# Four fronts of a graph-and-mixer network on one core: norms computed in halves, nodes transposed token tile by token tile, first products in two halves of the tokens

## The chip, the core and the metric

The kernel runs on one core of a Trainium2 chip, in one launch. The metric is the device time of one execution in microseconds (us): of the kernel before, 3632.74 as the median of three (3631.09 to 3634.49). The engines are TensorE (PE for its matmuls, PEld for its weight loads), VectorE (DVE), ScalarE (ACT), GpSimd (POOL) and SyncE (SP); each has its own queue of instructions, and semaphores join them. DMAs are issued on the queues of SP and POOL.

## What is computed

A network of four layers works on 512 nodes of 768 features, in float32, with 8704 edges. Each layer is

```
xn = layernorm(x)
x  = x + graph_net(xn, edges) + mixer(xn)
x  = x + ffn(layernorm(x))
```

The graph nets, mixers and FFNs of the four layers are of different kinds. What matters here:

- **Mixer of layer 0** (8 heads of 96 features, 256 random features `rf`): `phi(q) = exp(q rf^T - |q|^2 / 2)`, the same for k, then `phi(q) (phi(k)^T v)` over `phi(q) sum(phi(k))`, and a projection. `|q|^2` and `|k|^2`, one number per node and head, are the "norms" of this text.
- **Mixer of layer 1** (12 heads of 64): the same form; its first products are those of v.
- **FFN of layer 1**, a dense block: `gelu(xn W1^T + b1) W2` with 384 hidden features.
- **Layer 3**: a graph attention of 12 heads of 64, narrow because all heads share one 64 x 64 weight `W_fc` and one `W_res`; and a linear mixer with 768 queries, keys and values, normalized along the tokens, and a projection. Its FFN has 16 experts, each of which takes its 64 best nodes, with gate, up and down weights of 768 x 3072, and a shared block.

## The kernel before, in words

x stays in SBUF as 4 token tiles of 128 nodes (`NT` = 4). A product over features needs the nodes with the features on the partitions: `xnT`, 6 chunks of 128 features by 512 nodes (`KC` = 6, `N` = 512). PE makes them by transposes of 128x128, and DVE or ACT copy them out of PSUM. PSUM has eight banks of 128x512 floats, handed out in turn by `ps()`.

A planner sets the order of each engine's queue: the order of the Python code is the priority, and of two instructions the earlier one goes first unless its inputs are ready later by the planner's own clock. So a piece of Python code that is run "beside" another, by a generator that is advanced by one step per product, lands between that code's instructions. `issue_after` adds an order by hand. Weights come on SP's queue (`w`, L299), into six rotating buffers in most stages. Small loads come on POOL's.

Helpers: `copy` (L286 to L292) gives copies to DVE (L290) and ACT (L292) in turn; `acc` (L429) is a row of accumulating matmuls; `tr` (L450) is one transpose; `norm1` (L505 to L517) the layernorm of one token tile: two bn_stats, aggregate, square root on ACT, reciprocal, and a scaling on DVE of 128x768. `add_x` (L522) adds a product of 128x384 to x on DVE.

`to_fm` (L457 to L464) turns the nodes: token tile by token tile, 24 transposes into six banks, one per chunk of features, then six copies of 128x512. Each copy needs the transposes of all four tiles, and a product needs all six copies. It is called for the second mixer (L2799), in the dense block (L1958) and for the last layer (L2300).

**First mixer** (`mix0`, L817). Its 8 heads go in two groups g of four. Products of the first layers are made from slices of float32 split in parts (rounded on ACT by `cut`, L2069, and the rest), for accuracy. For each group `heads3` makes the keys of four heads by four products (48 matmuls) and calls a function beside the first three of them, then the same for the queries. `norms` (L847 to L858) handles four heads: ACT squares (L852) and rounds (L2069), DVE subtracts (L854), PE sums over the 96 features by two matmuls per head (L856), and four copies (L858) put the rows into row 96 of `qk`, where the later products pick them up. The keys' norms are run as one piece beside the first query product; the queries' norms come behind all query products and the `keys` of two heads (L860: matmuls with `rf`, exponentials on ACT). Then `queries` (L870) and the rest of each head go in a pipeline. `part` and `sq` have two buffers.

In group 0, between the products of keys and queries, stands `checked` (L687 to L704), which looks whether the graph's counts are in the expected bounds: two DVE reductions, a row of matmuls for the degrees (`deg`), 4 times two DVE instructions which add the degrees to the diagonal of `AT`, then one small product `ones` by `check` and four more small DVE instructions (L700 to L704), the last of which writes `big`. SP loads `big` into registers (L923) in group 1; a branch later depends on it.

**Second mixer** (`mix1`): after `to_fm` at L2799 and the short `turn`, the products of v are made by token tiles: for weight block 4, then 5, all six chunks of one token tile at a time.

**Dense block** (`ffn1`, L1952): norm, `to_fm`, then three chunks of hidden features, each by six matmuls of 512 columns over six chunks (the trace has 36 matmuls, as each is done in two passes), GELU on ACT, and the second product.

**Last layer** (`last_two`, L2291). After `to_fm`, `gnn3` (the graph attention, L2380) is created as a generator of 41 steps, and its opening runs at once: loads on POOL's queue (among them the block-diagonal `bd` of `W_fc` and `W_res`), the narrow product of the attention's vectors `V`, 24 products of nodes with `bd` and their copies. Its other steps are advanced by two per product. The products are `fm(m3_wqkv, ...)`: nbs 0 to 3 are queries and keys, 12 products of 512 columns, each followed by `put` (L2310: ACT copies with sums, and two steps of `gnn3`); then the queries are scaled, nbs 4 and 5 are the values (6 products), and the projection goes by token tiles, two products of 384 columns per tile, with two steps after each. Where the generator has ended, the rows of the finished tiles are normed and written to DRAM (L2352, L2353), from where the experts' nodes are fetched.

The experts' weights use SP's queue from the end of `last_two` on: `ffn3` (L2461) takes some of its buffers from the SBUF that `gnn3` used, so SP waits there for the last instruction of `gnn3` that reads this memory, `add` (L2445).

Of the kernel before, what the change touches and what calls it, by code (L numbers as in the profile page):

```python
# [10 lines left out]
F32 = mybir.dt.float32  # L11
BF16 = mybir.dt.bfloat16
F32R = mybir.dt.float32r
# [9 lines left out]
P = 128  # L23
N = 512
NT = N // P
D = 768
KC = D // P
HW = 384
# [177 lines left out]
class Net:  # L206
# [250 lines left out]
    def to_fm(self, x, out):  # L457
# [5 lines left out]
        for f in range(KC):  # L463
            self.copy(out[:, f, :], ps[f])  # L464

    def to_fm_last(self, x, out):

        nc, cut = self.nc, (NT - 1) * P
        ps = [self.ps() for _ in range(KC)]
# [3 lines left out]
        for f in (0, 1, 3, 4):  # L473
            i = nc.scalar.copy(out[:, f, :cut], ps[f][:, :cut])
# [3 lines left out]
        for f in range(0, KC, 3):  # L478
            p = self.ps()
# [5 lines left out]
            else:  # L485
                with self.tc.issue_after(i.ins):
                    i = nc.scalar.copy(*at)
# [80 lines left out]
    def counts(self, AT, EFT, deg, tmp, ones, meanwhile, then):  # L568
# [10 lines left out]
        with ExitStack() as c:  # L579
# [88 lines left out]
            for f in range(2):  # L668
                p = self.ps()
# [17 lines left out]
        def checked():  # L687
# [8 lines left out]
            for t in range(NT):  # L696
                at = slice(t * P, (t + 1) * P)
                nc.vector.tensor_mul(tmp, self.ident, deg[:, at])
                nc.vector.tensor_add(AT[:, t, at], AT[:, t, at].bitcast(F32), tmp)
            p = self.ps()  # L700
            self.acc(p[:, :5], [(self.ones, check)])
# [115 lines left out]
    def mix0(self, xnT, checked, ops, v, bv):  # L817
# [3 lines left out]
        with ExitStack() as c:  # L821
# [25 lines left out]
            def norms(qk, s):  # L847
                p = self.ps()
                for h in range(4):
                    sq = two.tile([96, N], F32, name="sq")  # L850
                    part = two.tile([96, 2, N], F32R, name="part")
                    nc.scalar.activation(sq, qk[:96, s, h, :], AF.Square)  # L852
                    self.cut(part[:, 0], sq)
                    nc.vector.tensor_sub(part[:, 1], sq, part[:, 0].bitcast(F32))  # L854
                    for i in range(2):
                        nc.tensor.matmul(p, half[:, 96 - 32 * h : 224 - 32 * h], part[:, i], start=h + i == 0, stop=h + i == 4)  # L856
                for h in range(4):
                    self.copy(qk[96:97, s, h, :], p[32 * h : 32 * h + 1])  # L858
# [62 lines left out]
            for g in range(2):  # L921
                if g:
                    loads, (self.wrong,) = nc.values_load_multi_w_load_instructions(self.big[:1], min_val=0, max_val=1)  # L923
                qk = one.tile([97, 2, 4, N], F32, name="qk")
                self.heads3(d["m0_wqkv"][2 + g, 0], ops, qk[:96, 1], sb[:, KC + 3 * g : KC + 3 * g + 3], scale,
                            lambda i: next(left, None))
                if g == 0:
                    checked()
                self.heads3(d["m0_wqkv"][g, 0], ops, qk[:96, 0], sb[:, 3 * g : 3 * g + 3], scale,
                            lambda i: norms(qk, 1) if i == 0 else None)  # L930
                fks = [keys(qk, 0), keys(qk, 1)]
                norms(qk, 0)
                fq = queries(qk, 0)
# [1018 lines left out]
    def ffn1(self):  # L1952
        nc, tc, d = self.nc, self.tc, self.d
        with tc.tile_pool(name="f1", bufs=1) as one:
            xn = one.tile([P, NT, D], F32, name="xn")
            xnT = one.tile([P, KC, N], F32, name="xnT")
            self.norm(self.x, xn)
            self.to_fm(xn, xnT)  # L1958
            w1, w2 = self.wk(d["f1_w1"]), self.wr(d["f1_w2"])
            hT = one.tile([P, 3, N], F32, name="hT")  # L1960
            for f in range(3):
                p = self.ps()
                self.acc(p, [(w1[:, k, f * P : (f + 1) * P], xnT[:, k, :]) for k in range(KC)])
                nc.scalar.activation(hT[:, f, :], p, AF.Gelu, bias=self.col("f1_b1", f))
# [326 lines left out]
    def last_two(self, xn, xnT, out, V):  # L2291
# [5 lines left out]
        with ExitStack() as c:  # L2297
            one = c.enter_context(tc.tile_pool(name="m3_one", bufs=1))
            two = c.enter_context(tc.tile_pool(name="m3_two", bufs=2))
            self.to_fm(xn, xnT)  # L2300
            beside = self.gnn3(c, xnT, V)
            next(beside)
            qk = one.tile([P, 2, KC, N], F32, name="qk")
# [16 lines left out]

            self.fm(d["m3_wqkv"], xs, put, nbs=(0, 1, 2, 3))
            nc.scalar.activation(rn, s[:, 1], AF.Sqrt)
# [413 lines left out]
def tile_net(ctx, tc, dram, at, out, only=ALL):  # L2736
# [51 lines left out]
    with tc.tile_pool(name="L1", bufs=1) as pool, ExitStack() as keep:  # L2788
# [9 lines left out]
        nc.gpsimd.memset(V1, 0.0)  # L2798
        net.to_fm(xn, xnT)  # L2799
        turn(V1, vt)  # L2800
# [51 lines left out]
```

## Time and profile before

| | before |
|---|---|
| median of 3 runs | 3632.74 us |
| the profiled execution | 3629.75 us |
| its span, first to last instruction | 3628.0 us |
| PE busy | 97% |
| DVE, ACT, POOL busy | 47%, 27%, 13% |
| granted TensorE clock, mean | 0.991 |
| DMA | 714.56 MB, mean 197 GB/s |

Where the four places lie in the span (us from its start):

| place | from | to | what the ends are |
|---|---|---|---|
| mixer 0, group 0: keys' products | 114.4 | 126.6 | matmuls of `heads3` |
| mixer 0, group 0: queries' products | 130.2 | 144.9 | matmuls of `heads3` |
| mixer 0, group 0: norms of the queries | | 153.5 | first matmul behind them |
| mixer 1: transposes | 939.6 | 946.8 | `to_fm` at L2799 |
| mixer 1: first product | 948.4 | | |
| dense block: transposes | 1491.8 | 1497.7 | `to_fm` at L1958 |
| dense block: first products | 1497.8 | 1513.5 | 36 matmuls |
| last layer: transposes | 2305.5 | 2313.4 | `to_fm` at L2300 |
| last layer: first product of `m3_wqkv` | 2330.0 | | |
| `gnn3` ends | | 2490.3 | `add`, L2445 |
| last layer: projection ends | | 2511.4 | |
| last matmul of the experts | | 3608.9 | |

How to read the views. A row of a timeline has the start and the length of an instruction or a group of like ones, engine, line and operation, output <- inputs, partitions x elements, how many (x4), and in brackets the idle time of the engine before it with the instruction that ended the wait. A row of the windows has the stretch, its length, then for PE, PEld, DVE, ACT and POOL the busy time and the number of instructions, the mean granted TensorE clock (1.00 is full speed), the mean busy share of the DMA engines and the GB/s that they moved. In a list of waits, the numbers are the total in us, how often, and the longest.

### The profile page before, as it was taken

The page shows a single profiled execution, that of the slowest core. Times are in us where ns is not written, and L with a number is a line of the kernel's source. Part 1 is how long each engine was busy: PE and PEld are TensorE (multiplying, and loading weights), DVE is VectorE, ACT ScalarE, POOL GpSimd, SP SyncE. Part 2 cuts the span into 40 slices and gives each one's busy share as a digit, 9 for nine tenths or more (in the row PEclk, how much of TensorE's full clock was granted, in tenths as well). Part 3 has the DMA queues.
Part 4 walks back from the last instruction along what each step waited for, and adds up shares of the span by engine and source line. Part 5 has one row for each costly group of instructions (what it writes and reads, how often), then busy time and mean ns, then how long its engine had stood idle before and what let it go on. Part 6 is the DMA issues. An engine that isn't in the chain of part 4 may idle for free.

```text
span 3628.0 us, 40612 instructions
## 1 busy us (share of the span) xinstructions
PE 3530.9 (97%) x15976; PEld 2208.5 (61%) x15981; DVE 1707.9 (47%) x3422; ACT 980.6 (27%) x1741; POOL 475.2 (13%) x522
## 2 busy tenths in 40 slices
PE   8999999999999999999999998999999999999998
PEld 6668666655586675587878785556444444444444
DVE  8647664653433662366777763476222221221211
ACT  2533332332342453142343432263000000000000
POOL 8211110012003010001221213111000000000000
PEclk9999999999999999999999998999999999999999
DMA  4213122228312120022121118415999999999998
GB/s 177 91 49 119 43 87 90 72 94 335 111 68 92 71 114 35 0 109 100 54 90 66 66 40 310 149 53 211 389 423 424 424 424 424 424 424 423 424 425 351
DMA packets 96988, 714.56 MB, mean 197 GB/s; under 512 B 11744, under 2 KB 12000, under 8 KB 27280
## 3 DMA queue, kind: packets, MB, share of 16 engines
q1 hardware_dynamic: 76032, 604.81, 41.3%
q0 software_dynamic: 16848, 95.99, 6.9%
q10 hardware_dynamic: 3904, 11.01, 0.8%
q8 instruction: 132, 2.16, 0.2%
q14 instruction: 72, 0.59, 0.0%
HBM read 689.22 MB, written 22.54 MB: 196 GB/s over the span
## 4 chain that ended last, share of the span: by engine, by line
PE 64%; DMA 5%; DVE 3%; issue 1%; ACT 0%; POOL 0%; POOLq 0%; DVEq 0%; SPq 0%; ACTq 0%
PE ps L429 29%; PE ps L2655 12%; PE ps L2671 7%; PE ps L2175 6%; PE ps L2626 3%; DMA w<-in_f_Wd_dram 2%; PE ps L450 2%; PE ps L1888 2%; PE ps L400 1%; DMA w<-in_f_Wg_dram 1%; DMA w<-in_f_Wu_dram 1%; PE ps L1869 1%; DVE pt L1598 1%; DVE e L1597 1%; DMA xb<-f_there,who 0%
## 5 line engine op out<-in xcount | busy, mean ns | idle before, releaser
L2655 PE MATMUL ps<-w,xg 128*64 128x384 f32 x3072 | 565.3, 489 | 7.7 <-DMA w<-in_f_Wg_dram 4.3
L2655 PEld LDWEIGHTS ps<-w,xg 128*64 128x64 f32 x3072 | 236.8, 137 | 295.6 <-issue 262.7
L429 PE MATMUL ps<-ops,w 128*128 128x512 f32 x1584 | 383.8, 392 | 0.0
L429 PEld LDWEIGHTS ps<-ops,w 128*128 128x128 f32 x1584 | 296.2, 188 | 63.6 <-issue 1.9
L2671 PE MATMUL ps<-w,hT 128*64 128x384 f32 x1536 | 320.6, 490 | 3.3 <-DMA w<-in_f_Wd_dram 1.9
L2175 PE MATMUL ps<-ops,w 128*128 128x512 f32 x1080 | 259.4, 390 | 1.3 <-DVE xn L2184 0.6
L2069 ACT ACTIVATE w<-w 128x768 fp32r<-128x768 f32 (+1 forms) x192 | 156.6, 825 | 355.9 <-PE ps L429 269.4
L2658 ACT ACTIVATE h<-ps 128x384 f32<-128x384 f32 x64 | 31.4, 491 | 795.8 <-PE ps L2655 795.8
L2671 PEld LDWEIGHTS ps<-w,hT 128*64 128x64 f32 x1536 | 134.3, 137 | 162.0 <-issue 136.3
L2175 PEld LDWEIGHTS ps<-ops,w 128*128 128x128 f32 x1080 | 201.9, 188 | 45.8 <-ACT ops L2088 1.7
L522 DVE TENSOR_TENSOR x<-x,ps 128x384 f32<-128x384 f32 x232 | 127.1, 552 | 188.9 <-PE ps L429 179.8
L2659 DVE TENSOR_TENSOR h<-h,ps 128x384 f32<-128x384 f32 x64 | 35.5, 554 | 354.4 <-PE ps L2655 345.8
L2113 DVE TENSOR_TENSOR w<-w,w 128x768 fp32r<-128x768 f32 x174 | 166.0, 957 | 65.1 <-ACT w L2069 61.8
L429 PE MATMUL ps<-w,xnT 128*128 128x384 f32 x564 | 189.4, 489 | 0.0
L429 PE MATMUL ps<-w,hT 128*128 128x384 f32 x552 | 184.6, 490 | 2.8 <-ACTq L1474 2.8
L2083 POOL TENSOR_TENSOR low<-low,ops 128x512 f32<-128x512 f32 x90 | 118.4, 1316 | 422.9 <-ACT ops L2069 422.9
L2114 DVE SCALAR_TENSOR_TENSOR w<-w 128x768 fp32r<-128x768 f32 x174 | 170.8, 984 | 3.2
L429 PEld LDWEIGHTS ps<-w,hT 128*128 128x128 f32 x552 | 103.1, 190 | 80.4 <-ACT xbT L292 7.1
L429 PEld LDWEIGHTS ps<-w,xnT 128*128 128x128 f32 x564 | 106.9, 191 | 73.5 <-issue 5.7
L2626 PE MATMUL ps<-xnT,sw 128*128 128x512 f32 x288 | 135.4, 603 | 0.0
L429 PE MATMUL ps<-C,parts 128*128 128x512 f32 x576 | 132.5, 389 | 0.0
L2090 DVE TENSOR_TENSOR ops<-ops 128x512 fp32r<-128x512 f32 x138 | 123.6, 906 | 16.4 <-ACT ops L2088 16.0
(585 smaller groups left out, 5188.8 us busy)
## 6 DMA issues: line engine op xcount, KB each, us to landing
w<-in_f_Wg_dram SPq DMA_DIRECT2D x128, 1152.0 KB, 22.5
w<-in_f_Wu_dram SPq DMA_DIRECT2D x128, 1152.0 KB, 22.4
w<-in_f_Wd_dram SPq DMA_DIRECT2D x128, 1152.0 KB, 22.4
w<-in_g_w_dram SPq DMA_DIRECT2D x54, 1152.0 KB, 5.1
w<-in_m_wqkv_dram SPq DMA_DIRECT2D x16, 1152.0 KB, 6.0
w<-in_g_t_dram SPq DMA_DIRECT2D x12, 1152.0 KB, 5.0
w<-in_m_wp_dram SPq DMA_DIRECT2D x11, 1152.0 KB, 5.0
ea<-in_attr_dram SPq DMA_DIRECT2D x17, 512.0 KB, 4.7
```

Source lines behind the costliest of these rows:

```text
L429: i = self.nc.tensor.matmul(out, a, b, start=n == 0, stop=n == len(pairs) - 1)
L450: return self.nc.tensor.transpose(out, in_, self.ident[:k, :k])
L522: self.nc.vector.tensor_add(xs, xs, p)
L2069: return self.nc.scalar.activation(top, x, AF.Copy, scale=CUT).ins
L2083: (engine or nc.gpsimd).tensor_sub(low, v, ops[:, 0, k, :].bitcast(F32))
L2090: nc.vector.tensor_sub(dif, top.bitcast(F32), x.bitcast(F32))
L2113: nc.vector.tensor_sub(low, w, top.bitcast(F32))
L2114: self.sliced_last = nc.vector.scalar_tensor_tensor(dif, low.bitcast(F32), -TIMES, top.bitcast(F32), OP.mult, OP.add).ins
L2175: nc.tensor.matmul(outs[o], w[:, i, k], ops[:, i, k, :], start=n == 0 and i + k == 0, stop=n == 4 and i + k == KC)
L2626: i = nc.tensor.matmul(p, w[:, k, :], xnT[:, k, :], start=k == 0, stop=k == KC - 1)
L2655: nc.tensor.matmul(p[a * 64 : a * 64 + 64, :HW], xg[:, k, a * CAP : (a + 1) * CAP], ws[b][a][:, k, :], start=k == 0, stop=k == KC - 1)
L2671: nc.tensor.matmul(po[nb][a * 64 : a * 64 + 64, :HW], hT[:, f * P + a * 64 : f * P + a * 64 + 64], wd[a][:, f, nb * HW : (nb + 1) * HW], s ...
```

## The change

`to_fm_tiles` stands in for `to_fm` at its three calls: each token tile is transposed in two groups of three chunks, and one copy of 128x384 follows each group, so that there are eight copies instead of six.

`in_halves` makes three output chunks of a product in three banks that are held together: first the first 256 tokens of all three, then the other 256. It replaces the first products of the dense block and the first block of `m3_wqkv`.

In `last_two` this first block is moved ahead of the opening of `gnn3`, with no steps of `gnn3` beside it; the other three blocks of queries and keys, the values and the projection advance it by two steps per product as before.

In the first mixer `norms` becomes a generator with two halves of two heads: squares, rounding and subtraction of a half, then a step, then its matmuls and the next half; the rows are copied at the end. The keys' norms are spread over the three calls beside the query products. The queries' first half, with its matmuls, and the squares, rounding and subtractions of their second half are issued ahead of the `keys` of two heads; the second half's matmuls and the row copies come behind them. `checked` becomes a generator as well: its second part (product, four small DVE instructions) goes behind the query products.

```diff
--- before.py
+++ after.py
@@ -462,6 +462,24 @@
                 self.tr(ps[f][:, t * P : (t + 1) * P], x[:, t, f * P : (f + 1) * P])
         for f in range(KC):
             self.copy(out[:, f, :], ps[f])
+
+    def to_fm_tiles(self, x, out):
+
+        for t in range(NT):
+            for f in (0, 3):
+                p = self.ps()
+                for k in range(3):
+                    self.tr(p[:, k * P : (k + 1) * P], x[:, t, (f + k) * P : (f + k + 1) * P])
+                self.copy(out[:, f : f + 3, t * P : (t + 1) * P], p[:, :HW].rearrange("p (k n) -> p k n", k=3))
+
+    def in_halves(self, w, xT):
+
+        ps = [self.ps() for _ in range(3)]
+        for h in range(2):
+            at = slice(h * N // 2, (h + 1) * N // 2)
+            for f, p in enumerate(ps):
+                self.acc(p[:, at], [(w[:, k, f * P : (f + 1) * P], xT[:, k, at]) for k in range(KC)])
+        return ps
 
     def to_fm_last(self, x, out):
 
@@ -697,6 +715,7 @@
                 at = slice(t * P, (t + 1) * P)
                 nc.vector.tensor_mul(tmp, self.ident, deg[:, at])
                 nc.vector.tensor_add(AT[:, t, at], AT[:, t, at].bitcast(F32), tmp)
+            yield
             p = self.ps()
             self.acc(p[:, :5], [(self.ones, check)])
             nc.vector.tensor_scalar(bad, p[:, :5], 0.0, None, OP.not_equal)
@@ -845,15 +864,23 @@
                 nc.scalar.mul(half[:, at], self.ones[:96, : at.stop - at.start], u)
 
             def norms(qk, s):
-                p = self.ps()
-                for h in range(4):
+                p, parts = self.ps(), []
+
+                def made(h):
                     sq = two.tile([96, N], F32, name="sq")
-                    part = two.tile([96, 2, N], F32R, name="part")
+                    parts.append(two.tile([96, 2, N], F32R, name="part"))
                     nc.scalar.activation(sq, qk[:96, s, h, :], AF.Square)
-                    self.cut(part[:, 0], sq)
-                    nc.vector.tensor_sub(part[:, 1], sq, part[:, 0].bitcast(F32))
-                    for i in range(2):
-                        nc.tensor.matmul(p, half[:, 96 - 32 * h : 224 - 32 * h], part[:, i], start=h + i == 0, stop=h + i == 4)
+                    self.cut(parts[h][:, 0], sq)
+                    nc.vector.tensor_sub(parts[h][:, 1], sq, parts[h][:, 0].bitcast(F32))
+
+                for hs in ((0, 1), (2, 3)):
+                    for h in hs:
+                        made(h)
+                    yield
+                    for h in hs:
+                        for i in range(2):
+                            nc.tensor.matmul(p, half[:, 96 - 32 * h : 224 - 32 * h], parts[h][:, i], start=h + i == 0,
+                                             stop=h + i == 4)
                 for h in range(4):
                     self.copy(qk[96:97, s, h, :], p[32 * h : 32 * h + 1])
 
@@ -924,12 +951,18 @@
                 qk = one.tile([97, 2, 4, N], F32, name="qk")
                 self.heads3(d["m0_wqkv"][2 + g, 0], ops, qk[:96, 1], sb[:, KC + 3 * g : KC + 3 * g + 3], scale,
                             lambda i: next(left, None))
+                of_keys = norms(qk, 1)
                 if g == 0:
-                    checked()
+                    check = checked()
+                    next(check)
                 self.heads3(d["m0_wqkv"][g, 0], ops, qk[:96, 0], sb[:, 3 * g : 3 * g + 3], scale,
-                            lambda i: norms(qk, 1) if i == 0 else None)
+                            lambda i: next(of_keys, None))
+                next(check, None)
+                of_queries = norms(qk, 0)
+                next(of_queries)
+                next(of_queries)
                 fks = [keys(qk, 0), keys(qk, 1)]
-                norms(qk, 0)
+                next(of_queries, None)
                 fq = queries(qk, 0)
                 for h in range(4):
                     hh = g * 4 + h
@@ -1955,12 +1988,10 @@
             xn = one.tile([P, NT, D], F32, name="xn")
             xnT = one.tile([P, KC, N], F32, name="xnT")
             self.norm(self.x, xn)
-            self.to_fm(xn, xnT)
+            self.to_fm_tiles(xn, xnT)
             w1, w2 = self.wk(d["f1_w1"]), self.wr(d["f1_w2"])
             hT = one.tile([P, 3, N], F32, name="hT")
-            for f in range(3):
-                p = self.ps()
-                self.acc(p, [(w1[:, k, f * P : (f + 1) * P], xnT[:, k, :]) for k in range(KC)])
+            for f, p in enumerate(self.in_halves(w1, xnT)):
                 nc.scalar.activation(hT[:, f, :], p, AF.Gelu, bias=self.col("f1_b1", f))
             for t in range(NT):
                 for nb in range(2):
@@ -2297,9 +2328,8 @@
         with ExitStack() as c:
             one = c.enter_context(tc.tile_pool(name="m3_one", bufs=1))
             two = c.enter_context(tc.tile_pool(name="m3_two", bufs=2))
-            self.to_fm(xn, xnT)
-            beside = self.gnn3(c, xnT, V)
-            next(beside)
+            self.to_fm_tiles(xn, xnT)
+            beside = iter(())
             qk = one.tile([P, 2, KC, N], F32, name="qk")
 
             s = one.tile([P, 2, 2, KC], F32, name="s")
@@ -2318,7 +2348,11 @@
                 for _ in range(2):
                     next(beside, None)
 
-            self.fm(d["m3_wqkv"], xs, put, nbs=(0, 1, 2, 3))
+            for f, p in enumerate(self.in_halves(self.wk(d["m3_wqkv"][0, 0]), xnT)):
+                put(f, p)
+            beside = self.gnn3(c, xnT, V)
+            next(beside)
+            self.fm(d["m3_wqkv"], xs, put, nbs=(1, 2, 3))
             nc.scalar.activation(rn, s[:, 1], AF.Sqrt)
             nc.vector.reciprocal(rn, rn)
             nc.vector.tensor_mul(c0, s[:, 0], rn)
@@ -2796,7 +2830,7 @@
         space = right.tile([P, NT * 12 * 65], F32, name="va")
         V1 = pool.tile([P, KC, 32], F32, name="V1")
         nc.gpsimd.memset(V1, 0.0)
-        net.to_fm(xn, xnT)
+        net.to_fm_tiles(xn, xnT)
         turn(V1, vt)
         aT = net.mix1(space, xnT)
         with ExitStack() as e:
```

## Prediction

> **What bounds the kernel now.** I read the page first.
>
> ```profile
> PE 3530.9 (97%) x15976; PEld 2208.5 (61%) x15981; DVE 1707.9 (47%) x3422; ACT 980.6 (27%) x1741; POOL 475.2 (13%) x522
> ...
> PEclk9999999999999999999999998999999999999999
> ...
> PE 64%; DMA 5%; DVE 3%; issue 1%; ACT 0%; POOL 0%; POOLq 0%; DVEq 0%; SPq 0%; ACTq 0%
> ```
>
> PE is the bound of nearly every stage; the engines beside it are half idle on average. What can be had is PE idle time and half-speed clock around short chains. Then the busy time by windows at the end of the kernel (share of the DMA engines and GB/s are the last two columns):
>
> ```profile
> 2530.00:2550.00 20.00, 18.69 (x85) 9.20 (x84) 8.93 (x22) 0.97 (x2) 1.11 (x3) 1.00 0.65 252
> 2550.00:2570.00 20.00, 19.26 (x95) 8.28 (x94) 7.30 (x32) 1.09 (x2) 0.54 (x1) 1.00 0.97 385
> 2570.00:2590.00 20.00, 20.00 (x114) 8.74 (x114) 5.82 (x18) 0.97 (x2) 1.54 (x2) 1.00 0.97 389
> 2590.00:2610.00 20.00, 20.00 (x124) 12.58 (x122) 3.38 (x6) 1.46 (x3) 0.00 (x0) 1.00 1.01 427
> ```
>
> From 2590 on the stream of expert weights fills the DMA engines (1.01, 424 to 427 GB/s) to 3600: these 1000 us take no gain. A gain ahead of 2490 reaches the end only as far as the stream starts earlier.
>
> **1. Norms of the first mixer.** PE alone, group 0 (start, length):
>
> ```profile
> 150.58 0.50 PE L856 MATMUL ps<-part,half 96*128 96x512 f32 x1 [1.31 <-ACT part L2069]
> 151.30 1.10 PE L856 MATMUL ps<-part,half 96*128 96x512 f32 x3 [0.22 <-DVE part L854]
> 153.54 3.78 PE L429 MATMUL ps<-qk,rf 97*128 97x512 f32 x4 [1.14 <-DVE qk L290]
> 157.12 3.18 PE L429 MATMUL ps<-fk,v 128*97 128x256 f32 x8
> 160.13 1.88 PE L429 MATMUL ps<-qk,rf 97*128 97x512 f32 x4
> ```
>
> PE waits 1.31 + 0.22 + 1.14 = 2.67 us in the queries' norms, and then runs the same four matmuls in 3.78 that take 1.88 later, eight in 3.18 against 1.89: 3.2 lost to a slow clock. Group 1 has waits of 0.32 + 1.17 + 0.49 + 0.77 = 2.75 and 3.15 of slow clock. The windows agree on the clock (column before the last two):
>
> ```profile
> 146.00:150.00 4.00, 3.27 (x15) 2.47 (x13) 1.02 (x2) 3.99 (x8) 0.00 (x0) 1.00 0.00 0
> 150.00:154.00 4.00, 2.06 (x5) 1.13 (x6) 3.38 (x5) 3.00 (x6) 0.00 (x0) 0.86 0.00 0
> 154.00:160.00 6.00, 6.00 (x12) 3.00 (x12) 3.08 (x4) 1.87 (x4) 0.00 (x0) 0.52 0.00 0
> ...
> 940.00:944.00 4.00, 1.99 (x15) 1.38 (x14) 3.86 (x14) 1.62 (x3) 1.61 (x4) 1.00 0.67 272
> 944.00:948.00 4.00, 2.79 (x14) 2.20 (x14) 1.73 (x7) 2.95 (x6) 0.00 (x0) 0.60 0.00 0
> 948.00:952.00 4.00, 4.00 (x10) 2.35 (x9) 3.71 (x7) 4.00 (x9) 0.00 (x0) 0.55 0.01 4
> ```
>
> After the change a group's last query product is followed by the keys' second half (4 matmuls, 0.9), the queries' first half, both key blocks (16 matmuls, 3.62), the queries' second half. The second half's chain is cut 0.63, two subtracts of 0.69, matmul 0.5, row copy 0.68 and hand-overs of about 0.6: 3.8 us, half of it under key matmuls. But `part` has two buffers, so the queries' first squares now wait for the keys' last matmuls, and the keys' row copies (0.68 on DVE, 0.57 on ACT) stand in the same queues. Counting forward I get some 7.5 us with 5.4 of PE work: waits of 2.0 in group 0 (0.7 gained) and 1.5 in group 1 (1.2), where DVE has no check to do. Bounds: nothing stays (5.4 gained); ACT, with 9.3 us of work in these 7.5, makes it 1 worse. Clock: 0 to 6.3; I take one group's, 3.2, as the waits become scattered.
>
> The Trainium skill (TensorE: Matmul & The Clock Gate, HAM oscillation) speaks against that last gain: it has the clock fall only after idle gaps beyond about 3.4 us. No wait here is over 1.31, and yet the granted clock is 0.52, so the row decides; by the rule the 3.2 would be left out.
>
> The check's wait on `deg` (2.13 of PE at 127.9) goes behind the query products, with its two matmuls and four small DVE instructions. What is late next is DVE: the first query slice's low part is done at 130.84, and DVE is busy for 5.4 of 6 us until 146. Of 2.13 I take 0.5 (0 to 2.1). `big` comes some 12 us later; SP loads its registers from it only near 180. Term 1: 0.7 + 1.2 + 3.2 + 0.5 = **5.6** (-1 to 13.8).
>
> **2. Second mixer.** PE:
>
> ```profile
> 942.84 0.87 PE L450 MATMUL ps<-ident,xn 128*128 128x128 f32 x6 [1.00 <-ACT xn L1511]
> 943.55 0.75 PE L450 MATMUL ps<-ident,vt 96*128 96x96 f32 x6
> 945.25 1.54 PE L450 MATMUL ps<-ident,xn 128*128 128x128 f32 x6 [0.95 <-ACT xn L1511]
> ```
>
> Products start at 948.39, slow at first, and end at 980.66. With a copy per three transposes, the first token tile is transposed from 939.5 (six in 0.87) and copied by 941.1 (ACT 0.48, DVE 0.56 for 128x384). From there PE owes 8 x 4.03 of products, 18 transposes (2.6) and the 0.75: 35.6, so 976.7, a gain of 4.0. The eight copies (0.52 on average) cost 0.5 more than six of 0.57 to 0.63, and DVE, busy 3.86 of 4 us with the norms, may put its copies last: then nothing is gained and 0.5 lost. At 935.08 a weight slice of a later step got into that same DVE chain, so ready work does slip in: I take **3.0** (-0.5 to 4.0).
>
> **3. Dense block.** PE idles 2.15 + 0.49 + 0.13 between 1493.27 and 1497.79, where 36 matmuls of 512 columns take 15.72. Halves are 72 of 256 columns; 36 of that size take 8.02 at 2322, so 16.04: 0.3 dearer. If half one starts at 1493.9, with 12 transposes (1.75) in between, it ends at 1511.7 instead of 1513.5: 1.8. DVE's copies behind the norms (done at 1496.73) would make it -0.3. ACT copies chunks 0 to 2 in time: **1.4**.
>
> **4. Opening of the last mixer.** The first block's products start at 2329.97 and would end 15.9 later, 2345.9. After: 12 transposes 1.7, block 16.0, narrow product 2.5, 48 matmuls with `bd` 10.7, the rest 2.1: 33.1 us from when two tiles are copied. t1 is transposed at 2308.5; copies land at 2309.6, or 2310.8 behind the norms: ends at 2342.7 to 2343.9, later by up to 1.7 if the clock falls as it does now (0.57 in 2310 to 2314). The 1.52 wait for `bd` goes under the block. **2.0** (0 to 3.2).
>
> **5. The graph network ends later.** It has 41 steps. Now step 1 is the opening, 36 ride on 18 products, 38 to 41 on the first projection tile. After, 30 ride on 15 products, and 40 and 41 on the first half of the third tile: three half tiles (4.04 each) later, 12.1 us. SP's queue waits for that end:
>
> ```profile
> SPq L299 <- DVE x L2445: 26.0, 1, 26.0
> ```
>
> At 2491.2 it lets five expert weights go. The stream would start 12.1 later against the products. Idle DMA left in the first table: 0.36 x 20 + 2 x 0.04 x 20 = 8.8 us (by GB/s against 424: 11.6). So 0.5 to 3.3 is lost, 12.1 if the idle time can't be used; I take **-2.0**. POOL's loads of shared weights (now 2490.6, used at 2520) and three row writes move with it; the norms of tiles 0 to 2 (some 2.2 each on DVE) fit under the last 8 us of products.
>
> **Sum.** 5.6 + 3.0 + 1.4 + 2.0 - 2.0 = 10.0 off the profiled execution's 3629.75 (span 3628.0): 3619.75. The median shown is 3.0 above that execution, so 3622.7.
>
> **Rivals.**
> - More: clock full in both groups, all copies on time, idle DMA takes the late start: 9.7 + 4.0 + 1.8 + 3.2 - 0.5 = 18.2, 3614.5. For it: DVE and ACT average 47% and 27%. Against: both are full exactly there. 0.2.
> - The change doesn't overlap what it says: copies queue behind norms, or a product waits for all tiles, since a copy spans three chunks; the clock falls as before. 1.9 + 0.5 + 0 + 0.5 - 2 = 0.9: 3632. 0.2.
> - Slower: the weights' late start. If the idle DMA at 2534 to 2546 isn't filled (the first expert step itself comes late), 12.1 stands against fronts of 2.9: +9, 3642. It decides once the start is later than the 8.8 of idle time plus what the fronts gave. 0.1.
>
> **Numbers.** My case has 0.5 (own range 3617 to 3629). A measurement tells 0.2%, 7.3 us, from no change: my case is faster with 0.4 and same with 0.1; "more" adds 0.2 to faster, "doesn't overlap" 0.2 to same, "slower" 0.08 to slower and 0.02 to same: faster 0.60, same 0.32, slower 0.08. The range takes in the first two rivals with some room for the bounds; 3642 is left out.
>
> **What would show it.** Granted clock at 150 to 160 near 1; L856 waits under 2 per group; mix1's first product near 942, ffn1's near 1494, both among transposes; the 12-matmul groups there as 256 columns; SP's burst some 10 us nearer to the last transposes, and DMA share at 1 in the 20 us after. I am wrong if the fronts come earlier by their sum but the last expert product doesn't, or if the waits of the first mixer's norms get longer and ACT ends them.

## The result, and the profile after

The changed kernel takes 3638.26 us (median of 20 runs, 3632.73 to 3643.17) against 3631.07 us of the kernel before (20 runs): a ratio of 1.0017, with a 95% interval of 1.0011 to 1.0024. The forecast was 3622.7, and 3638.26 lies above its range. The profiled execution of the changed kernel has a span of 3636.5 us, 8.5 more than that of before. Lines of the page of after:

```profile
span 3636.5 us, 40765 instructions
PE 3533.7 (97%) x16048; PEld 2226.3 (61%) x16053; DVE 1707.3 (47%) x3425; ACT 981.3 (27%) x1744; POOL 475.8 (13%) x522
PE 31%; DMA 5%; DVE 1%; ACT 0%; issue 0%; POOL 0%; DVEq 0%; SPq 0%; ACTq 0%; POOLq 0%
```

PE is 2.8 us busier and idles some 5.7 us more; nothing on this page says where. So the two traces are laid side by side by anchors, points that both have (the first transpose of a front, the end of its products), and the length of each stage is taken. In these two executions:

| stage, from where to where on PE | before | after | difference |
|---|---|---|---|
| start to mixer 1's first transpose | 939.58 | 936.83 | -2.75 |
| mixer 1: first transpose to end of the v products | 41.08 | 43.84 | +2.76 |
| from there to the dense block's first transpose | 511.14 | 511.06 | -0.08 |
| dense block: first transpose to end of its first products | 21.55 | 21.62 | +0.07 |
| from there to the last layer's first transpose | 792.13 | 792.85 | +0.72 |
| last layer: first transpose to end of the projection | 205.89 | 211.92 | +6.03 |
| from there to the first expert product | 27.01 | 29.16 | +2.15 |
| first expert product to the end of the span | 1089.62 | 1089.22 | -0.40 |

The sum is +8.5. The row with +0.72 holds no changed code: a wait of 1.36 for a DMA (`yb`) is gone there, and some 2 us went between 1830 and 2292 with hardly any wait longer than before, by a slower clock behind the same waits. Such differences come and go between executions: the 14 kernels of this document, one profiled execution each, have the same code in this stretch and take 791.6 to 795.7 for it. Further down the stages are therefore averaged over all profiled executions that share their code.

**First mixer.** PE in group 0 of after, as in the timeline shown of before:

```profile
142.72 0.50 PE L882 MATMUL ps<-part,half 96*128 96x512 f32 x1 [0.38 <-ACT part L2100]
144.34 1.13 PE L429 MATMUL ps<-rf,qk 97*128 97x256 f32 x4 [1.12 <-DVE qk L290]
149.12 0.49 PE L882 MATMUL ps<-part,half 96*128 96x512 f32 x1 [0.31 <-ACT part L2100]
150.16 1.13 PE L882 MATMUL ps<-part,half 96*128 96x512 f32 x2 [0.54 <-DVE part L874]
152.90 3.48 PE L429 MATMUL ps<-qk,rf 97*128 97x512 f32 x4 [0.78 <-DVE qk L290]
156.18 2.13 PE L429 MATMUL ps<-fk,v 128*97 128x256 f32 x8
```

The check's wait of 2.13 is gone, but the waits around the norms have not become less: with one more of 0.34 they sum to 3.5 (2.67 before). In this sum is a new one of 1.12, that of the keys for their own norms' row copies. The first four products of queries still take 3.48.

**Second mixer and dense block.** PE in after (before, the products are `948.39 32.73` and `1497.79 15.72`, and the tiles are transposed from 939.58 on and from 1491.80 on):

```profile
936.83 0.87 PE L450 MATMUL ps<-ident,xn 128*128 128x128 f32 x6 [0.24 <-ACT xn L1544]
940.68 0.87 PE L450 MATMUL ps<-ident,xn 128*128 128x128 f32 x6 [2.97 <-ACT xn L1544]
943.33 1.54 PE L450 MATMUL ps<-ident,xn 128*128 128x128 f32 x6 [1.77 <-ACT xn L1544]
945.72 1.54 PE L450 MATMUL ps<-ident,xn 128*128 128x128 f32 x6 [0.85 <-ACT xn L1544]
948.02 33.12 PE L429 MATMUL ps<-w,xnT 128*128 128x384 f32 x96
...
1495.44 0.85 PE L450 MATMUL ps<-ident,xn 128*128 128x128 f32 x6 [2.24 <-DVE mv L532]
1497.12 0.84 PE L450 MATMUL ps<-ident,xn 128*128 128x128 f32 x6 [0.84 <-DVE xn L535]
1497.81 15.71 PE L429 MATMUL ps<-xnT,w 128*128 128x256 f32 x72
```

This is the heart of the result. The tiles are transposed and copied one by one, and the halves are there (72 matmuls of 256 columns), but in PE's queue all 24 transposes stand ahead of the first product. In the second mixer PE waits for the norms of the second, third and fourth tile (2.97, 1.77, 0.85), while products of the first, copied by 938.31, lie ready behind these waits. In the dense block it waits 2.24 and 0.84; there half of the copies of the first two tiles, ACT's, are done by 1493.39, the other half, DVE's, stand in the norms' chain until 1496.39. The granted clock (the column before the last two) in the second mixer falls as before:

```profile
936.00:940.00 4.00, 1.46 (x8) 0.64 (x6) 3.88 (x11) 1.95 (x4) 1.75 (x4) 1.00 0.79 307
940.00:944.00 4.00, 1.54 (x9) 1.31 (x10) 3.54 (x13) 2.72 (x5) 0.00 (x0) 0.72 0.00 0
944.00:948.00 4.00, 3.15 (x17) 2.75 (x16) 1.29 (x4) 2.62 (x5) 0.00 (x0) 0.50 0.02 4
948.00:952.00 4.00, 4.00 (x9) 2.18 (x8) 3.23 (x6) 3.74 (x9) 0.00 (x0) 0.50 0.00 2
```

DVE is 3.88 and 3.54 of 4 us busy: the copies of 128x384 have gone into the chain of the norms, and each tile's norm is later by what was put ahead of it. The fourth tile's transposes start 8.89 us behind the first's, 7.48 before.

**Last layer.** `pt` are the weights of the edges, which DVE makes for each head of the graph attention; from the one-hots (`oh`) come the numbers of an expert's nodes. Rows of PE around a wait for each, then rows of what lies behind the two waits (the scalings of the queries on DVE; the last row write and the one-hots):

```profile
2428.24 0.44 PE L429 MATMUL ps<-ft,pt 128*128 128x65 f32 x2 [1.97 <-DVE pt L1631]
2428.84 4.84 PE L429 MATMUL ps<-ft,pt 128*128 128x65 f32 x26 [0.17 <-DVE pt L1631]
2434.34 6.52 PE L429 MATMUL ps<-xnT,w 128*128 128x512 f32 x12
...
2536.47 0.74 PE L429 MATMUL ps<-number,oh 128*128 128x2 bf16 x4 [1.66 <-DVE oh L2597]
```
```profile
2413.12 8.11 DVE L2367 SCALAR_TENSOR_TENSOR qk<-qk,f 128x512 f32<-128x512 f32 x6
...
2521.25 14.75 DMA f_there<-xn
2536.08 0.90 DVE L2597 TENSOR_TENSOR oh<-io,above 128x128 bf16<-128x128 int16 x4 [2.20 <-DMA f_there<-xn]
```

Before, the first wait was 0.17, and the products behind it ran at full clock:

```profile
2437.27 3.12 PE L429 MATMUL ps<-ft,pt 128*128 128x65 f32 x26 [0.17 <-DVE pt L1598]
2440.66 5.31 PE L429 MATMUL ps<-xnT,w 128*128 128x512 f32 x12
```

SP's wait for the end of the graph network, 26.0 before, is now

```profile
SPq L299 <- DVE x L2479: 50.0, 1, 50.0
```

so the five expert weights go at 2510.1 in place of 2491.2. The idle time of the DMA engines behind that has been used up (share and GB/s are the last two columns):

```profile
2530.00:2550.00 20.00, 16.98 (x62) 8.16 (x62) 10.87 (x28) 5.15 (x11) 2.87 (x4) 1.00 1.01 425
2550.00:2570.00 20.00, 19.35 (x101) 8.33 (x97) 6.78 (x26) 1.58 (x3) 0.54 (x1) 1.00 1.01 420
2570.00:2590.00 20.00, 19.91 (x103) 8.81 (x105) 8.02 (x32) 0.97 (x2) 1.54 (x2) 1.00 0.99 403
```

From this alone one could put all 8.5 us down to the late stream. The experiments say otherwise.

### The profile page after: what moved, and what is told of

It is laid out like the page before. It is cut to its first block, busy times and chain, and to the rows that moved or that the text cites. A ratio compares the mean times of both kernels' runs of the same rounds, so it can differ in the third digit from the quotient of the medians.

```text
span 3636.5 us, 40765 instructions
## 1 busy us (share of the span) xinstructions
PE 3533.7 (97%) x16048; PEld 2226.3 (61%) x16053; DVE 1707.3 (47%) x3425; ACT 981.3 (27%) x1744; POOL 475.8 (13%) x522
## 3 DMA queue, kind: packets, MB, share of 16 engines
q1 hardware_dynamic: 76032, 604.81, 41.3%
```

## Experiments

Each was timed side by side with the kernel before; the numbers in brackets are the 95% interval of the ratio. A length of a stage in a single run is that of one profiled execution. "Theory Q" is: the parts cost by the order in which instructions stand in the queues. Its rivals are named in the expectations.

### The change without its last part: `fronts_no_last`

The last layer as before, all else as changed; against the changed kernel:

```diff
-            self.to_fm_tiles(xn, xnT)
-            beside = iter(())
+            self.to_fm(xn, xnT)
+            beside = self.gnn3(c, xnT, V)
+            next(beside)
...
-            for f, p in enumerate(self.in_halves(self.wk(d["m3_wqkv"][0, 0]), xnT)):
-                put(f, p)
-            beside = self.gnn3(c, xnT, V)
-            next(beside)
-            self.fm(d["m3_wqkv"], xs, put, nbs=(1, 2, 3))
+            self.fm(d["m3_wqkv"], xs, put, nbs=(0, 1, 2, 3))
```

> The change without its part in the last layer. Theory Q (the parts cost by the order of queues): in the changed kernel's trace PE is 2.3 us ahead after the first mixer, and has lost that again when the second mixer's first products end (980.67 against 980.66), and the dense block gives 0. So nothing is left: ratio 1.000, mixer 1's products of queries and keys start near 980.7. Rival A (the second mixer's tiles cost nothing by themselves, and something fixed in time ended the stage): they start at 978 and the ratio is 0.9994. Either way the 7 us that the whole change costs are not here.

Ratio 0.9999 (0.9990 to 1.0008): the loss isn't here. The interval takes in Rival A's 0.9994 too. The absolute point of the expectation was a bad measure (this execution came into the second mixer 4.5 us earlier, at 932.36); the length of the stage is the right one, 43.18 against 41.08. So Rival A falls: the tiles cost by themselves.

### Only the last part: `last_alone`

The same lines the other way round, on the kernel before.

> Only the last layer's part of the change, on the kernel before. Theory Q: the copies stretch the norms ahead of the transposes (+2.0), the graph network's late steps meet the scaling of the queries on DVE (a wait near 2428 and a slow clock, +4), the row writes land behind the weights (+2): 3639, ratio 1.002, SP's burst some 19 us later than 2491. Rival S (only the late stream costs): the same ratio, but PE is no more than 2 us late when the projection ends, 2511 to 2513.

Ratio 1.0033 (1.0022 to 1.0044), no less than the whole change. Transposes to projection end 211.88, from there to the first expert 29.21, as in the changed kernel. PE is 4.65 late at the projection's end, 2516.02, though it came to the first transpose 1.34 earlier: rival S falls.

### The move without the tiles: `last_move`

As `last_alone`, but with one line of before:

```diff
-            self.to_fm_tiles(xn, xnT)
+            self.to_fm(xn, xnT)
             beside = iter(())
```

> Only the move in the last layer: the first block of products ahead of the graph network's opening, without steps beside it; the nodes are transposed as before, by chunks. Theory Q (copies, and the move, cost separately): transposes end as before (2313.4), the wait for bd is gone (-1.5), the wait near 2426 with its slow clock is there (+4 to +5), the late row writes too (+2): about +5 at the first expert product, ratio 1.0014. Rival C (the tiles are what costs, the move is free): ratio 1.000.

Ratio 1.0022 (1.0013 to 1.0030). Transposes to projection end 209.50 (206.3 is the mean of the kernels with the old order), from there to the first expert 29.78. The wait near 2426 is there and is 1.97 again, so Rival C falls: the move costs by itself. The tiles cost some 2.4 on top of it (211.88 less 209.50); 1.9 of that is in the transposes, from the first of them to the first product 9.64 against 7.75. Both are single executions, the timed intervals overlap, and the old order alone spreads from 204.3 to 209.7, so this split is rough.

### The stream held: `stream_late` and `stream_held`

In the kernel before, the fifth expert weight is held until the third tile's second projection product is added. The first try gave the planner an order (`issue_after`) to keep:

```diff
                 i, self.taken = self.taken % 15, self.taken + 1
+                if self.taken == 5:
+                    self.fed, self.early = self.late, 1
```

> The kernel before, but SP's burst of expert weights is held until the third token tile's second projection product is added to x, 12.9 us later than now (2504 in place of 2491); PE's work and order as before. Theory P (the end follows PE at the first experts, the stream has room): 0 to 1 us, ratio 1.000. Theory S (the end follows the stream's start, less the idle time of the DMA engines that it can use, 8.8 to 11.6 us): +1.3 to +4.1, ratio 1.0004 to 1.0011. If the idle time can't be used: +12.9, ratio 1.0036.

SP went on at the end of the graph network all the same (2492.64), so this run told nothing but the spread: ratio 1.0004 (0.9995 to 1.0013) for a kernel that does the same. The second try added a dependence with a semaphore, by the means that the kernel has for its other expert layers (`w`, L299, adds it to the fifth load from there):

```diff
+                    if (t, nb) == (2, 1):
+                        self.gate, self.before = i.ins, 4
```

> The kernel before, with the first of the five expert weights truly held by a semaphore until the third token tile's second projection product is added (in the run before, the added order moved nothing: SP went on at the end of the graph network). The stream starts some 12.9 us later, at 2504; PE's work and order as before. Theory P (the stream has room, the end follows PE at the first experts): 0 to 1 us, ratio 1.000 to 1.0003, the first expert product still near 2538. Theory S (the end follows the stream's start less the 8.8 to 11.6 us of idle time): +1.3 to +4.1, ratio 1.0004 to 1.0011. If the idle time can't be used: +12.9, ratio 1.0036.

```profile
2507.13 0.81 SPq L299 DMA_DIRECT2D w<-in_f_Wg_dram  x2
2507.99 1.08 SPq L299 DMA_DIRECT2D w<-in_f_Wu_dram  x2
```
```profile
2530.00:2550.00 20.00, 18.68 (x88) 9.21 (x87) 7.93 (x18) 1.97 (x4) 2.33 (x3) 1.00 0.98 397
```

The projection ended at 2513.98 in this execution (2.6 later than before, for reasons ahead of it), so the stream came 13.3 us later against PE. The DMA engines had no idle time to speak of (0.98), and yet the first expert product was 27.01 behind the projection's end, and the span's end 1088.91 behind that: both as before. Ratio 1.0002 (0.9993 to 1.0011), so these lengths speak for theory P: a start some 13 us later costs nothing that can be seen. The timed interval takes in theory S's 1.0004 to 1.0011 as well and excludes only the 1.0036. One more thing stands in this trace: the last of the four row writes goes out at 2517.11, 10.0 us behind the burst, and lands in 7.4 us.

### More steps beside the values: `last_dense`

On the changed kernel:

```diff
-                for _ in range(2):
+                for _ in range(2 + (a == 2)):
                     next(beside, None)
```

> The changed kernel, but with three steps of the graph network beside each of the six products of values in place of two, so that it ends some three products (about 12 us) earlier against PE. Theory Q: the row writes come ahead of the weights again, the wait of 1.66 for the one-hots goes, and the stream starts earlier: 2 to 5 us off the changed kernel, 3633 to 3636, ratio to before 1.0005 to 1.0013; the wait near 2428 stays. Rival D (DVE is too full there): PE waits for the edges' weights at each product, over 3 us more, ratio 1.0025 or more.

Ratio 1.0024 (1.0015 to 1.0033). Both theories are right in half. The wait for the one-hots is gone (27.00 from projection to experts), but PE pays for it in the heads:

```profile
2429.96 0.66 PE L429 MATMUL ps<-ft,pt 128*128 128x65 f32 x2 [7.85 <-DVE pt L1631]
```

### The scalings spread: `last_spread`

On the changed kernel:

```diff
                 if a == 2:
+                    scaled(f)
                     nc.vector.tensor_mul(qk[:, 0, f, :], qk[:, 0, f, :], p)
...
-            for f in range(KC):
+            def scaled(f):
                 q, k = qk[:, 0, f, :], qk[:, 1, f, :]
```

> The changed kernel, but the six scalings of queries (1.35 us each on DVE, 8.1 in a row) stand each ahead of the value product that uses it. Theory Q (the scalings in a row meet the graph network's first heads because its steps come six products later): the wait of 1.97 near 2428 and the slow clock behind it go, the projection ends 4 to 5 us earlier than in the changed kernel (near 2513.5), ratio to before 1.0005 to 1.001. Rival E (heads at this place are limited by DVE whatever the scalings do): the same wait, moved by a product or two, ratio 1.0017 as in the changed kernel.

Ratio 1.0008 (0.9999 to 1.0017). No wait for `pt` is left, and from the end of the rows' stall (a wait of 3.54 for `rows`, at 2394.52 in the changed kernel and the same in both) to the projection's end it takes 118.8 in place of 123.6: the 4.8 were the scalings in a row. Rival E falls. The wait for the rows' write stays (31.17 to the experts).

### The check alone: `check_only`

The kernel before with the second part of `checked` (a generator as in the change) behind the query products:

```diff
-                    checked()
+                    check = checked()
+                    next(check)
...
+                next(check, None)
                 fks = [keys(qk, 0), keys(qk, 1)]
```

> The kernel before, with only the second part of the check moved behind the query products; the norms as before. If the 2.3 us that the changed kernel gains in the first mixer all come from the check, PE reaches the first products of layer 0's graph network 2 us earlier (256.9 becomes about 254.9), ratio 0.9994. If the halves of the norms carry a part of it, less than 1.2 us is gained here, ratio 0.9997 or more.

Ratio 0.9990 (0.9981 to 0.9999). From the degree product to the last transposes of the mixer's result 121.47 us; six executions of the old code have 123.9 to 126.1, mean 124.5. So the check alone gives 3.0 in this execution, and 2.7 between the medians. Seven executions with the norms in halves as well have 118.7 to 122.0, mean 121.0: the halves add 0.5, less than their own spread.

### PE's order by hand: `hand_order`

The kernel before with tiles in the second mixer and the dense block, where `issue_after` puts the transposes of a tile behind products of earlier ones:

```diff
+                i = self.acc(p[:, :HW], pairs)
+                if first and t < NT - 1 and nb == 4:
+                    first(t + 1, i.ins)
...
+                if h == 0 and f == 1:
+                    self.to_fm_tiles(x, xT, (2, 3), i.ins)
...
+            self.tm(d["m1_wqkv"], xs, put_v, nbs=(4, 5), first=lambda t, i: self.to_fm_tiles(xn, xnT, (t,), i))
             self.operands(ops, lambda k: (xnT[:, k, :], self.rest(), None), nc.vector)
-            self.tm(d["m1_wqkv"], xs, put_v, nbs=(4, 5))
```

The last lines also move the v products ahead of `operands`, which splits `xnT` for the products that follow them.

> The kernel before with tiles in the second mixer and the dense block, but PE's order written by hand: in the second mixer the transposes of a token tile stand behind the product of the tile before, in the dense block those of tiles 2 and 3 behind two thirds of the first half. Theory Q: products start near 941.5 and end near 976.7 (-4.0); the dense block ends at 1511.7 less that (-1.8): 5.8 us gained, ratio 0.9984. Rival B (the copies behind the norms on DVE and ACT are what costs, whatever PE's order): -1 or nothing, ratio 0.9997 to 1.000.

Ratio 0.9983 (0.9974 to 0.9992). PE in the second mixer:

```profile
941.22 4.06 PE L431 MATMUL ps<-w,xnT 128*128 128x384 f32 x12
945.12 0.82 PE L452 MATMUL ps<-ident,xn 128*128 128x128 f32 x6
946.54 4.14 PE L431 MATMUL ps<-w,xnT 128*128 128x384 f32 x12 [0.61 <-ACT xnT L292]
950.51 0.82 PE L452 MATMUL ps<-ident,xn 128*128 128x128 f32 x6
```

First transpose to end of the products: 35.98 (41.08 before, 43.84 changed); in the dense block 19.08 (21.55, 21.62). The copies sit in the same DVE chain as in the changed kernel: in the dense block DVE's first one starts 3.60 us behind the first transpose in both. Yet the products start 1.71 behind it in place of 6.08:

```profile
1488.93 5.86 PE L431 MATMUL ps<-xnT,w 128*128 128x256 f32 x24 [0.24 <-ACT xnT L292]
```

So rival B falls: what cost was PE's order. The copies still delay the norms, but with products among the transposes PE has work meanwhile. The move of `operands` wasn't run by itself; its splits start behind the copies of the last tile in both kernels (ACT's at 947.26 changed, 956.91 here), and the dense block, where nothing of the kind moved, gains as well.

### Better versions: `best_a`, `best_c`, `best_d`

`best_a` joins the norms in halves, the late check and `hand_order`, and leaves the last layer as it was.

> The kernel before with the first mixer's norms in halves, and with tiles and PE's order by hand in the second mixer and the dense block; the last layer as before. Theory Q: gains of 2.3, 4.6 and 1.8 add up and reach the end, since the graph network ends earlier by as much and lets the stream go: -8.7 us, ratio 0.9976. Rival: the stream gives part of it back, ratio 0.9985.

Ratio 0.9959 (0.9945 to 0.9972). Each stage gained at least what was expected (mixer 0 121.1, mixer 1 36.0, dense block 19.1) and the profiled span is 8.9 us shorter, so its rival, a stream that gives a part back, falls. The timed runs gained more, 13.4 between the medians; the profiled execution is the slowest of the five, and where the rest lies isn't shown. `best_c` orders the last layer by hand too and spreads the scalings:

```diff
-            for f, p in enumerate(self.in_halves(self.wk(d["m3_wqkv"][0, 0]), xnT)):
+            for f, p in enumerate(self.in_halves(self.wk(d["m3_wqkv"][0, 0]), xn, xnT)):
```

> The version with the norms in halves and PE's order by hand in the second mixer and the dense block, and now also in the last layer: the first block's products among the transposes, then the opening of the graph network, and the scalings spread. Theory Q: the front gains 4 to 5 us against the version without it, the late row writes cost 2 to 3 (the stream comes 12 us later ahead of them): -1 to -3 us against that version, ratio to before 0.995 to 0.9975. Rival F (the late stream has no room left, once PE is ahead): 2 to 5 us slower than that version.

Ratio 0.9955 (0.9942 to 0.9969), median 3612.86 us. Its front takes 199.4 to the projection's end (206.6 in `best_a`) and gives back 4 for the late row writes. By the intervals it can't be told from `best_a`, so neither the gain of theory Q nor Rival F is settled; both versions beat both kernels. `best_d` adds the denser steps of `last_dense`:

> The version with PE's order by hand in all three places and the scalings spread, and now three steps of the graph network beside each value product, so that it ends about 12 us earlier against PE. In the runs so far the stretch from the projection's end to the first expert product is 27.0 us where the rows are written ahead of the weights and 31.1 where not. Theory Q: 27.0 to 28 here, the stretch before it is not longer than 199.4 by more than 1: 3 us off the version without it, ratio to before 0.994 to 0.996. Rival D (DVE is too full beside the value products): PE waits there for the edges' weights, the stretch before grows by 4 or more, ratio 0.996 to 0.998.

Ratio 0.9979 (0.9970 to 0.9988): rival D. The row writes are in time (27.01), but six waits for `pt` and a clock of 0.74 from 2420 to 2440 make the front 214.1.

## The prediction, point by point

The lengths over all profiled executions that share the code of a stage (us; the number of executions in brackets):

| stage | old code | changed | by hand | forecast gain | measured gain |
|---|---|---|---|---|---|
| mixer 0, degree product to last transposes | 124.5 (6) | 121.0 (7) | | 5.6 | 3.5 |
| mixer 1, transposes to end of v products | 40.8 (6) | 43.1 (4) | 36.0 (4) | 3.0 | -2.3 |
| dense block, transposes to end of first products | 22.1 (6) | 23.4 (4) | 19.1 (4) | 1.4 | -1.3 |
| last layer, transposes to projection end | 206.3 (7) | 211.9 (2) | 199.4 (1) | 2.0 | -5.6 |
| projection end to first expert product | 27.1 (7) | 29.2 (2) | 31.1 (1) | -2.0 | -2.1 |

The measured gains sum to -7.8, beside the -7.2 of the medians. Between the forecast's 10.0 and this lie 17.8 us: 8.0 in the second mixer and the dense block, 7.6 in the last layer up to the projection's end, 2.1 in the first mixer and 0.1 behind the projection.

Single executions spread. Mixer 1 takes 40.3 to 41.3 with the old code, 42.4 to 43.8 changed, and 35.98 to 36.02 by hand. In the dense block 21.5 to 23.0 (old) and 21.6 to 24.5 (changed) overlap, so there a loss isn't shown, only that nothing was gained; by hand it is 19.08 to 19.09. The last layer's old code takes 204.3 to 209.7.

**1. Norms of the first mixer: sign right, reasons not.** The check was mis-sized: 0.5 in the forecast, 3.0 measured (one execution). The argument that DVE would be late next did not hold. The halves were to give 5.1 by shorter waits and a full clock, and gave 0.5. In group 1 PE's waits behind the last query product are 0.36 + 1.12 + 0.35 + 0.78 = 2.61 (2.75 before), and the slow clock only moved: the 16 key matmuls now take 6.45 in place of 3.62, the eight `fk,v` 1.89 in place of 3.14. The wait of the keys' products for the keys' own rows (1.12) was not counted. The count of "some 7.5 us with 5.4 of PE work" was short as well: the four pieces it lists add up to 6.3, and from the keys' second half to `queries` the trace has 11.8 (group 0) and 13.1 (group 1). That the total of 3.5 comes near 5.6 is luck.

**2. and 3. Second mixer and dense block: the failed step.** It is "From there PE owes 8 x 4.03 of products, 18 transposes", and "with 12 transposes in between" for the dense block. Both took it that products would go among the transposes once a tile was copied. The traces of after show PE waiting for a transpose while products stood behind it whose tiles (in the dense block, half of their chunks) were copied: the queue had the transposes first, and nothing passed them. The prediction named this as a rival ("The change doesn't overlap what it says") with 0.2, by other causes and at a gain of 0.9; that the copies in the norms' chain make such a front longer than before was bounded at -0.5 and came to -2.3. What the planner expected of the norms when it chose that order is in no trace and stays open; that the order is the cause of the missing gain is shown by `hand_order`, which reached 4.8 and 3.0, more than the bounds of the forecast. One reason for the excess is in the rows of `hand_order`: at a clock of 1.00 from 936 to 960, the twelve matmuls of a product take PE 3.90 until the next piece starts (941.22 to 945.12), where the forecast counted their whole length, 4.03.

**4. Opening of the last mixer.** The wait for `bd` went as forecast. But the transposes took 9.9 in place of 7.9, for the same reason as above, so that to the end of the rows' stall nothing was gained: 88.32 from the first transpose, less the 15.7 of the three products (36 matmuls of 512 columns) that now come ahead of it, against 72.44.

**5. The graph network's later end: terms put at nothing.** The delay was forecast well (12.1 against PE; SP's burst came 18.9 later, of which PE's own lateness is 6.75), and its price by the stream was not: nothing in the trace of `stream_held`. That the row's -2.1 meets the forecast's -2.0 is luck, since it is another cost. Two effects were missing from the sum, and they are the step that failed here. The scalings of the queries, 8.1 us of DVE in a row, meet the first heads (5.6 in the pair of traces: a wait of 1.97 and three groups at a slow clock). `last_spread` shows the cause.

And three tiles' row writes go out together behind the burst (2513.2 to 2515), the fourth, at 2521.25, takes 14.75 us, and the one-hots wait for it. They read nothing of these rows; in the code their pool opens where that of `xn`, from which the rows are written, has just closed, so it is probably the memory that they wait for. The burst alone doesn't do that: in `stream_held` the fourth write went out 10.0 behind it, here 11.2, and took 7.4. What is new beside it is POOL's own queue, where four loads of shared weights, three row writes and one more load stand between 2509.45 and 2515.65, ahead of the fourth write; in `stream_held` the first four loads left at 2493 to 2495. All five profiled kernels with the late end and two steps per product have 14.4 to 15.1. How the delay divides between the burst and POOL's own transfers was not run and stays open.

The statement that the norms of tiles 0 to 2 "fit under the last 8 us of products" looked at DVE alone, not at their DMAs. The rival that ended on the slow side had the right sign by the wrong mechanism: it blamed the stream. The rival "More" is summed with 9.7 for the first mixer, where 0.7, 1.2, 6.3 and 0.5 give 8.7; nothing hangs on it.

From the first expert product to the end it takes 1088.2 to 1089.6 in 13 of 14 profiled executions (1091.1 in one): the end followed PE at the first expert, also where the stream came late.

## What to carry to other kernels

A finer cut gives overlap only if the queue of the waiting engine lets the next work by: look at the order in which transposes and products stand in PE's queue before counting what could run between them, and write that order by hand if a planner sets it. When a piece of work is moved past others that are advanced beside it, look for the one long burst on a helper engine (here the 8 us of scalings) that its steps will now meet. Compare stages by their lengths between anchors and over several executions, not by absolute times of two traces.

## What the runs showed of the hardware

The granted clock fell to 0.50 behind waits of 0.35 to 2.97 us, and behind the same waits not in every execution: in the dense block, behind waits of 2.24 and 0.84, the 72 matmuls took 15.71 in the changed kernel at a clock of 1.00 (1498 to 1506) and 17.99 in `fronts_no_last`, at 0.63 from 1494 to 1500; both run the same code there. The Trainium skill (TensorE: Matmul & The Clock Gate, A second HAM failure mode: psum-queue depth-cycling) tells of a bf16 kernel whose frequent short idle times between groups of matmuls made the clock swing; this fits these rows better than its rule on gaps beyond 3.4 us, which the prediction weighed.

The six scalings of 128x512 took 1.35 each on DVE in a row beside POOL's products of the same tiles (10.09 for six), and 0.75 each when spread. The Trainium skill (GPSIMD Engine Reference, Key points) says that GpSimd shares its SBUF interfaces with VectorE and contends with instructions that read two SBUF inputs; the two durations agree with it.
